# Second pass's loads of tokens and normed tokens issued by GpSimd instead of SyncE

## The chip, the cores and the metric

The kernel runs on one core of one Trainium2 chip. The metric is the device time of one execution in microseconds (us). Of the kernel before the change three timed executions are shown, 3959.48 to 3974.03 us, with a median of 3963.63 us, and one further execution that the hardware profiler recorded.

## What is computed

The reference takes `x`, 32 images of 56 x 56 tokens with 128 channels in f32, through two "metaformer" layers, each a token mixer and an expert stage with residual adds:

```python
x = x + conv(_ln_c(x))          # batch norm over all tokens, sign, 3x3 convolution with signed weights
t = t + moe(_ln_t(t))           # 8 experts, the two with the highest gate, weighted by their gates
x = x + triangle(_ln_c(x))      # sigmoid products a, b per image; z = einsum(a, b); norm; gate
t = t + choice(_ln_t(t))        # 64 experts, each takes its 8 best tokens of an image and adds to them
```

The first mixer normalizes each token, then needs a mean and a variance over all tokens of all images. So the work has two passes over `x`: the first finds these sums, the second does everything else.

## The kernel before

**Tiling.** A unit is 896 tokens, a tile of 128 partitions x 7 x 128 f32 (448 KB). There are 112 units, 7 for each of 16 pairs of images.

**First pass.** SyncE loads each unit (L1552), DVE and ACT normalize it, PE transposes it and sums up its squares (L1594), and SyncE stores the transposed normed tokens to `y1_d` (L1585).

**Second pass**, in the terms of one pair of images:

- `fetch` loads a unit's tokens `x_` from the input again (L557). They stay in one of 12 slots "x" until the pair is done with them; the slot comes free when the last stage has read the tile and stored it to the output (`out<-x`, on ACT's queue).
- `sign` loads the unit's normed tokens `ys` back from `y1_d` (L565) into one of 5 slots "u", which many other tiles share; DVE compares them with a limit per channel and writes signs into a padded frame (L572).
- `conv` runs 9 matmuls per half unit on that frame (L594), ACT scales them (L602), PE turns them back (`trc`), and DVE adds them to `x_` (L536). This add is the first reader of the tokens.
- `moe_stats`, `moe_turn`, `moe_route` and `moe_gates` normalize the tokens, turn them, work out the eight gates of each token, and store the gates of a unit to HBM (`gate<-gT`, L769, on ACT's queue).
- `moe_experts`, once for each of a unit's 7 groups of 128 tokens: SyncE loads the group's 8 x 128 gates from HBM, broadcast to all 128 partitions (`gb`, 512 KB, L782, 784 of them, 5 slots "gb"); DVE multiplies them with the turned tokens (L788); PE multiplies the product with the eight experts' weights and sums up (L793); DVE adds the result to the tokens (L805).
- The triangle stage (L817 to L1037) and the last norm follow; ACT stores the finished tokens and the last norm's output `y3`; `top8` picks 8 tokens for each of 64 experts, and GpSimd gathers them from `y3` with 8 indirect DMAs for each pair (L1154, 64 KB each), which DVE sums up (L1172, L1174).

**Tail.** Once all pairs are routed, the 64 experts run on the chosen tokens; their weights come on SyncE's queue (L1319, L1323), and GpSimd adds the results into the output with 128 indirect DMAs in a row (L1418).

**Order.** All stages are entered in a list by `put` with a time each. The class `Order` then plays the list through with estimated durations, gives each operation to an engine when it is ready and a slot is planned to be free, and so fixes the order of the instructions of every engine. `@op("SP", 360, ..., land=1200)` enters an operation as one of SyncE's with its cost; the function under it issues the instruction, which may name another engine. On the chip each engine, SyncE and GpSimd included, goes through its own instructions in order: a DMA whose slot isn't free yet holds up the DMAs behind it on that engine.

Of the kernel before, what the change touches and what calls it, by code (L numbers as in the profile page):

```python
# [252 lines left out]
def kernel(ctx: ExitStack, tc: tile.TileContext, a: dict, out: bass.AP):  # L253
    nc = tc.nc
# [26 lines left out]
    def units(ap):  # L281

        return ap.rearrange("(u p n) c -> u p n c", p=128, n=N7)

    x_units = units(x.rearrange("b h w c -> (b h w) c"))
# [68 lines left out]
    y1_d = [dram.tile([C, N7, 128], F32, name=f"y1_{g}") for g in range(NUT)]  # L354
# [17 lines left out]
    with ExitStack() as c2:  # L372
# [26 lines left out]
        def new(tag, shape, name, dtype=F32):  # L399
            return op.tile(pools.get(tag, work), tag, shape, dtype, name)  # L400

        def unit_tile(name):
            return new("u", [128, N7, C], name)
# [4 lines left out]
        def parts(t, n=N7):  # L408
            return [(t, k) for k in range(n)]
# [4 lines left out]
        def rows_of(u):  # L414

            r0 = 16 * u
            if r0 < H < r0 + 16:
                return ((0, r0, H - r0, 0), (1, 0, r0 + 16 - H, 8 * (H - r0)))
            return ((r0 // H, r0 % H, 16, 0),)

        def bands(p, u):

            for h in range(2):
                img, r = divmod(2 * u + h, N7)
                yield ("frame", (2 * p + img) % NF, r)
# [125 lines left out]
        def fetch(p, u):  # L551
            g = p * NU + u
            x_ = live[p]["x", u] = new("x", [128, N7, C], f"x_{NUT + g}")

            @op("SP", 360, w=parts(x_), land=1200)
            def _():
                nc.sync.dma_start(x_.ap, x_units[g])  # L557

        def sign(p, u):
            g = p * NU + u  # L560
            y = unit_tile(f"ys_{g}")

            @op("SP", 360, r=[("y1_d", g)], w=[y], land=1200)
            def _():
                nc.sync.dma_start(y.ap, y1_d[g])  # L565

            keys = list(bands(p, u))
            for img, r0, nr, p0 in rows_of(u):
                @op("DVE", 80 + 60 * nr, r=[y, "bn"],
                    w=keys[: nr // 8] if p0 == 0 else keys[-(nr // 8) :])  # L570
                def _(img=img, r0=r0, nr=nr, p0=p0):
                    nc.vector.tensor_scalar(  # L572
                        frames[(2 * p + img) % NF][:, 1 + r0 : 1 + r0 + nr, 1 : 1 + W].rearrange(
                            "c r (v n) -> c r v n", n=N7
                        ),
                        y.ap[:, :, p0 : p0 + 8 * nr].rearrange("c n (r v) -> c r v n", v=NV),
                        bn_scale, bn_limit, ALU.mult, ALU.is_ge,
                    )
# [1319 lines left out]
```

## Time and profile before

| | us |
|---|---|
| median of 3 executions | 3963.63 |
| the profiled execution | 3960.44 |
| its span, first to last instruction | 3958.7 |
| PE busy (matmul) | 3579.1 (90%) |
| DVE busy | 3205.5 (81%) |
| ACT busy | 2318.1 (59%) |
| GpSimd (POOL) busy | 411.9 (10%) |
| DMA queue q1: 673.15 MB | 50.4% of 16 engines |
| DMA queue q10: 109.20 MB | 7.0% |
| DMA queue q0, software: 17.32 MB | 3.0% |

The first pass lasts until about 310 us, the second to about 3440 us, and the tail to the end. q1 is the queue that SyncE's DMAs use (it moves most of the bytes), and q0 the one of the indirect DMAs that GpSimd issues. In rows of the trace "PE acc L793 <- DVE gb L788: 51.3, 43, 3.0" says that PE stood before its instructions of line 793 until DVE's of line 788 were done, 51.3 us in all, 43 times, 3.0 us at the longest. "SPq" and "POOLq" are the issuing sequencers of SyncE and GpSimd. In a row of the timeline stand the start, the duration, the engine, the line, the operation and its tiles, and in square brackets the idle time before it and what ended it.

### The profile page before, as it was taken

The page shows a single profiled execution, that of the slowest core. Times are in us where ns is not written, and L with a number is a line of the kernel's source. Part 1 is how long each engine was busy: PE and PEld are TensorE (multiplying, and loading weights), DVE is VectorE, ACT ScalarE, POOL GpSimd, SP SyncE. Part 2 cuts the span into 40 slices and gives each one's busy share as a digit, 9 for nine tenths or more (in the row PEclk, how much of TensorE's full clock was granted, in tenths as well). Part 3 has the DMA queues.
Part 4 walks back from the last instruction along what each step waited for, and adds up shares of the span by engine and source line. Part 5 has one row for each costly group of instructions (what it writes and reads, how often), then busy time and mean ns, then how long its engine had stood idle before and what let it go on. Part 6 is the DMA issues. An engine that isn't in the chain of part 4 may idle for free. (4 is left out here: it accounts for less than half of the span.)

```text
span 3958.7 us, 77662 instructions
## 1 busy us (share of the span) xinstructions
PE 3579.1 (90%) x27571; PEld 2832.1 (72%) x27571; DVE 3205.5 (81%) x10496; ACT 2318.1 (59%) x5435; POOL 411.9 (10%) x441
## 2 busy tenths in 40 slices
PE   7998999999999999999999999999999999988563
PEld 6886877777777768686867777777777777765342
DVE  7997889898989888989898989888888898875311
ACT  5997356666656565656657574747474757454210
POOL 1000000001010101010101010101010101003657
PEclk8999999999999999999999999999999999988786
DMA  7996637474747465655556455656555555556784
GB/s 252 349 349 221 240 139 247 140 259 138 255 145 249 149 233 163 215 181 203 197 178 212 176 205 182 216 174 211 194 197 184 202 207 189 195 188 185 186 242 84
DMA packets 311396, 804.64 MB, mean 203 GB/s; under 512 B 71384, under 2 KB 95808, under 8 KB 311008
## 3 DMA queue, kind: packets, MB, share of 16 engines
q1 hardware_dynamic: 247888, 673.15, 50.4%
q10 hardware_dynamic: 41104, 109.20, 7.0%
q0 software_dynamic: 22016, 17.32, 3.0%
q8 instruction: 219, 3.59, 0.4%
q14 instruction: 169, 1.38, 0.1%
HBM read 629.33 MB, written 170.13 MB: 202 GB/s over the span
## 5 line engine op out<-in xcount | busy, mean ns | idle before, releaser
L793 PE MATMUL acc<-expert_w,gb 128*128 128x128 f32 x12544 | 1460.7, 278 | 56.0 <-DVE gb L788 51.3
L793 PEld LDWEIGHTS acc<-expert_w,gb 128*128 128x128 f32 x12544 | 1433.5, 194 | 99.1 <-DVE gb L788 65.2
L788 DVE TENSOR_TENSOR gb<-gb,xT 128x1024 f32<-128x1024 f32 x784 | 944.9, 1221 | 102.4 <-DMA gb<-gate 95.5
L449 DVE BATCH_NORM_STATS2 stln<-x 128x6 f32<-128x128 f32 x2352 | 587.3, 292 | 2.7
L1154 POOL DMA_INDIRECT rows<-y,near x128 | 182.9, 1429 | 3374.8 <-DMA gb<-gate 1444.0
L523 ACT ACTIVATE yl<-x,rmln 128x128 f32<-128x128 f32 x784 | 326.3, 492 | 213.2 <-DVE rmln L508 205.3
L594 PE MATMUL ps_cv<-frame,w_sign 128*128 128x448 bf16 x2016 | 423.1, 357 | 7.2 <-DVE frame L572 7.1
L523 ACT ACTIVATE yt<-x,rmln 128x128 f32<-128x128 f32 x784 | 324.3, 490 | 155.7 <-DVE rmln L508 151.7
L523 ACT ACTIVATE ym<-x,rmln 128x128 f32<-128x128 f32 x784 | 327.2, 496 | 92.4 <-DVE rmln L511 42.8
L594 PEld LDWEIGHTS <-w_sign 128*128 128x128 bf16 x2016 | 195.0, 98 | 189.1 <-issue 27.3
L1418 POOL DMA_INDIRECT out<-eo_False,picked x128 | 195.9, 1531 | 162.5 <-DMA out<-eo_False,picked 84.7
L995 PE MATMUL ps_g<-yT,wg 128*128 128x448 f32 x448 | 206.7, 566 | 1.7 <-DVE x L536 1.7
L523 ACT ACTIVATE y<-x,rm 128x128 f32<-128x128 f32 x448 | 196.2, 493 | 20.4 <-DVE rm L508 11.7
L544 ACT COPY xT<-trm 128x512 f32<-128x512 f32 x224 | 111.6, 543 | 158.3 <-PE trm L438 137.9
L449 DVE BATCH_NORM_STATS2 st<-x 128x6 f32<-128x128 f32 x784 | 182.1, 287 | 22.9 <-DMA x<-in_x 22.0
L1594 PE MATMUL gram<-y 128*128 128x128 f32 x1568 | 197.8, 279 | 0.0
L602 ACT ACTIVATE cv<-ps_cv,cv_shift,cv_scale 128x448 f32<-128x448 f32 x224 | 160.2, 725 | 60.3 <-PE ps_cv L594 53.0
L1594 PEld LDWEIGHTS gram<-y 128*128 128x128 f32 x1568 | 193.9, 199 | 0.0
L805 DVE TENSOR_TENSOR x<-acc,x 128x512 f32<-128x512 f32 x224 | 139.1, 621 | 65.3 <-PE acc L793 63.7
L1031 DVE SCALAR_TENSOR_TENSOR sg<-ps_zo,bz,sg 128x224 f32<-128x224 f32 x448 | 180.1, 450 | 13.3 <-PE ps_zo L1021 13.3
L1005 ACT ACTIVATE sg<-ps_g,bg 128x448 f32<-128x448 f32 x224 | 138.4, 634 | 83.5 <-PE ps_g L995 49.1
L438 PE MATMUL tr<-ident,y 128*128 128x128 f32 x784 | 140.6, 297 | 29.7 <-ACT y L523 24.6
(228 smaller groups left out, 5281.0 us busy)
## 6 DMA issues: line engine op xcount, KB each, us to landing
gb<-gate SPq DMA_DIRECT2D x784, 512.0 KB
x<-in_x SPq DMA_DIRECT2D x224, 448.0 KB
y<-yT SPq DMA_DIRECT2D x112, 448.0 KB
ys<-y SPq DMA_DIRECT2D x112, 448.0 KB
out<-x ACTq DMA_DIRECT2D x112, 448.0 KB
y<-yl ACTq DMA_DIRECT2D x112, 448.0 KB
w_False<-in_L_ffn_weight SPq DMA_DIRECT2D x128, 256.0 KB
w_True<-in_L_ffn_weight SPq DMA_DIRECT2D x48, 256.0 KB
```

Source lines behind the costliest of these rows:

```text
L438: nc.tensor.transpose(ps.ap[:, n * 128 : (n + 1) * 128], get()[:, n0 + n, :], ident)
L449: nc.vector.bn_stats(st.ap[:, c0 + k, :], src.ap[:, k, :])
L523: nc.scalar.activation(dst.ap[:, k, :], src.ap[:, k, :], AF.Identity, bias=m, scale=r)
L594: nc.tensor.matmul(acc, lhsT=w_sign[:, tap, :], rhs=frames[f][:, 8 * band + kh : 8 * band + kh + 8, kw : kw + W], start=(tap == 0), stop=( ...
L602: nc.scalar.activation(cv.ap[:, :, 64 * h : 64 * h + 64], ps.ap[:, :448].rearrange("c (q n) -> c n q", n=N7), AF.Identity, bias=cv_shift, ...
L788: nc.vector.tensor_tensor(gb.ap, gb.ap, over(xT.ap[:, n, :], E0), ALU.mult)
L793: nc.tensor.matmul(acc.ap[:, n % 4 * C : (n % 4 + 1) * C], lhsT=gb.ap[:, e, :], rhs=expert_w[:, e * C : (e + 1) * C], start=(e == 0), stop ...
L995: nc.tensor.matmul(psg.ap[:, :448], lhsT=wg, rhs=yT[:, H * img + r0 : H * img + r0 + 8, :].rearrange("c r w -> c (r w)"), start=True, stop ...
L1031: nc.vector.scalar_tensor_tensor(part, psz[q].ap[:, :224].rearrange("c (m v) -> c m v", v=2), bz, part, ALU.add, ALU.mult,)
L1154: nc.gpsimd.indirect_dma_start(out=rows.ap[:, j, :], out_offset=None, in_=y3_d[p], in_offset=bass.IndirectOffsetOnAxis(ap=near.ap[:, k + j ...
L1418: ins = nc.gpsimd.indirect_dma_start(out=tokens_out, out_offset=bass.IndirectOffsetOnAxis(ap=picked[lot][:rows, e : e + 1], axis=0), in_=e ...
L1594: nc.tensor.matmul(gram.ap[:, :C], lhsT=y.ap[:, n, :], rhs=y.ap[:, n, :], start=(g % G16 == 0 and n == 0), stop=(g % G16 == G16 - 1 and n ...
```

## The change

Two lines of the second pass change the engine that issues the load. The planner's entry for each stays as it was ("SP", 360, land=1200), so the planned order of all operations is the same; the 112 loads of `x_` and the 112 of `ys` stand in GpSimd's instruction order, among the 128 gathers of L1154, and no longer in SyncE's. SyncE issues the broadcasts of the gates, the small transfers of the routed tokens, and the last stage's weights.

```diff
         def fetch(p, u):
...
             @op("SP", 360, w=parts(x_), land=1200)
             def _():
-                nc.sync.dma_start(x_.ap, x_units[g])
+                nc.gpsimd.dma_start(x_.ap, x_units[g])
...
         def sign(p, u):
...
             @op("SP", 360, r=[("y1_d", g)], w=[y], land=1200)
             def _():
-                nc.sync.dma_start(y.ap, y1_d[g])
+                nc.gpsimd.dma_start(y.ap, y1_d[g])
```

## The prediction

> **What bounds the kernel now.** I read the stretches first, to find the part that the change can touch. The moved loads run from 310 us (first x load) to 3433 us (last one). The columns are the stretch, its length, then busy us of PE, PEld, DVE, ACT and POOL, the granted clock, the DMA share and GB/s.
>
> ```profile
> 1000.00:1600.00 600.00, 569.31 (x4495) 454.64 (x4493) 526.45 (x1630) 368.10 (x829) 36.70 (x24) 0.99 0.57 194
> 1600.00:2200.00 600.00, 565.01 (x4444) 450.43 (x4443) 523.06 (x1607) 366.48 (x829) 37.03 (x24) 0.98 0.58 197
> 3600.00:3959.00 359.00, 202.44 (x1255) 132.93 (x1253) 94.00 (x273) 69.28 (x130) 225.81 (x295) 0.76 0.72 187
> ```
>
> See: in the second pass PE works 565 to 570 of 600 us, DVE some 525, DMA 57%. PE is the bound, DVE close behind, and what can be won is PE's idle time: from 400 to 3440 us, 3040 less 2879 busy, **161 us**. The tail after 3600 us (POOL's scatters) holds none of the moved loads and only shifts.
>
> Next, who ends these idle times, and where SyncE's queue (SPq) stands, in the window 400 to 3440 us (us in total, times, longest):
>
> ```profile
> PE acc L793 <- DVE gb L788: 51.3, 43, 3.0
> PE trg L758 <- DVE gg L744: 19.9, 17, 1.6
> ...
> DVE gb L788 <- DMA gb<-gate: 86.0, 99, 3.2
> ```
>
> ```profile
> SPq L782 <- PE acc L793: 755.6, 433, 5.0
> SPq L782 <- DMA gate<-gT: 387.8, 57, 19.8
> SPq L557 <- ACT yl L523: 364.1, 77, 12.0
> SPq L782 <- DVE gb L788: 209.8, 77, 7.8
> SPq L557 <- DMA out<-x: 204.1, 32, 20.9
> SPq L565 <- PE trc L438: 135.3, 12, 13.8
> ```
>
> See: a third of PE's idle time is the chain broadcast (gb) late, DVE late, PE late; 51.3/86.0 = **0.60** of what DVE waits for gb arrives at PE. I use that share for every DVE wait below. SyncE stands over 1000 us at the moved loads (these rows and the smaller ones of L565), with gb's issues queued behind. But gb itself waits for one of its five slots (755.6 + 209.8 us) or for the gates' store (387.8 us), so most of that time a freed queue would only wait at its own head.
>
> **The change part by part.** PE's, DVE's and ACT's streams keep every instruction in the same order; 224 issues leave SyncE's queue and stand in GpSimd's, in their old order among themselves, between the 128 gathers of L1154. No byte is added.
>
> (1) *What gb gains.* I went through the timeline for each wait of DVE at L788 and noted what SyncE issued last before that gb. Behind another gb: 69.1 us, nearly all of it with the issue 0.03 us after the slot came free, so five slots and the transfer's own 4.6 us set it, not the queue. Behind an x load (L557): 26.0 us in 18 waits; behind a ys load (L565): 1.9 us. One of them:
>
> ```profile
> 1017.60 0.33 SPq L557 DMA_DIRECT2D x<-in_x  x1
> 1018.28 1.21 DVE L788 TENSOR_TENSOR gb<-gb,xT 128x1024 f32<-128x1024 f32 x1
> 1018.38 0.32 SPq L782 DMA_DIRECT2D gb<-gate  x1
> ...
> 1022.47 1.23 DVE L788 TENSOR_TENSOR gb<-gb,xT 128x1024 f32<-128x1024 f32 x1 [1.46 <-DMA gb<-gate]
> ```
>
> The gb goes out right behind an x load and DVE loses 1.46 us. If these 27.9 us go, PE wins 27.9 x 0.60 = **17 us**. At most all of L788's waits go: 51 us. At least it is a loss: the same bytes still share 16 DMA engines, and on two queues a gb that used to be ahead of a load now runs beside it. Queue q1 moved 673.15 MB in 50.4% of 16 engines' span, 337 GB/s, so a load of 448 KB is 1.36 us of all engines; 99 of the window's 753 gb are waited for (13%), so 200 loads x 1.36 x 0.13 x 0.60 = 21 us lost if each delays one gb by its whole length. I take 17, the row nearest to the matter; the ends are +51 and -21.
>
> The Trainium skill, DMA: Bandwidth & Descriptors, section Issuing engines are not separate DMA queues, speaks against the change: DMAs of any issuing engine run on the same 16 engines, and several issuers save only issue time. By it alone the sum would be the 224 issues of 0.33 us that SyncE no longer makes, at best a few us, since SyncE is no bound.
>
> (2) *What the moved loads lose.* A direct load issued by GpSimd is not in this trace. Nearest is its gather of 64 KB, against SyncE's x load of 448 KB where it is waited for:
>
> ```profile
> 1391.27 0.33 SPq L557 DMA_DIRECT2D x<-in_x  x1
> ...
> 1395.23 1.16 DVE L536 TENSOR_TENSOR x<-trc,x 128x512 f32<-128x512 f32 x2 [0.20 <-DMA x<-in_x]
> ```
>
> ```profile
> L1154 POOL DMA_INDIRECT rows<-y,near x128: 942/1018/4459, 696.7 to 3727.9; - x128
> ...
> DMA to landing us min/median/max: 2.5/3.4/6.0
> ```
>
> SyncE's load is there 3.96 us after its issue. A gather lands 2.5 / 3.4 / 6.0 us after it starts; 384 KB more at 337 GB/s add 1.2 us: 3.7 / 4.6 / 7.2 us. Load by load I took the time from issue to first reader (the add L536 for x, the frame pass L572 for ys): medians 48 and 9.9 us, but 15 x loads (about one a pair) have 3.95 to 6.9 us, and 23 ys loads 4.9 to 7.2 us. Those go out when their slot comes free, so a free queue does not help them. Summing what each lacks: landing at 3.7 us costs DVE nothing, at 4.6 us 3.1 us, at 5.4 us 12.4 us (ys 1.0, x 11.4), at 6.6 us 38.7 us, at 7.2 us 57.9 us. Times 0.60 at PE: 0 to **35 us**. I take 5.4 us, between median and worst because a gather's issue is often stretched (mean 1429 ns against a median of 1018): 7 us. The cover of the other 186 loads is the DVE work between issue and reader; without it each would cost what it lacks, as the 38 do.
>
> (3) *GpSimd's engine.* 224 issues of 1.43 us are 320 us on an engine that is busy 412 of 3959: free by itself. It can be held up, though:
>
> ```profile
> 1302.98 3.57 POOL L1154 DMA_INDIRECT rows<-y,near  x1 [0.31 <-issue]
> 1306.86 0.94 POOL L1154 DMA_INDIRECT rows<-y,near  x1 [0.30 <-issue]
> ```
>
> The 3.57 us one lies beside a run of L788 on DVE, the 0.94 us one beside two short DVE ops of 0.2 us. DVE's own ops do not suffer: L788 takes 1221 ns with and without a gather beside it. If the loads are stretched so, they land up to 2.6 us later, which is the 7.2 us end of (2) and is not added again.
>
> The Trainium skill, SBUF — State Buffer, section Who interferes with whom, says that a two-input VectorE op contends only with a GpSimd op that reads SBUF, and that the modes which would stop descriptor writing belong to copies and scalar ops. A gather reads its indices, a plain load reads nothing; by the rule the loads would keep the short issue and the landing stays near the median, a cost of 2 us. By the row alone it is up to 35.
>
> (4) *New order on GpSimd.* A load now stands behind gathers, which wait for the choice of rows (near) and the y3 stores. With the times of this trace only 5 of 224 loads went out before a gather that is now ahead of them, by 2.3 to 4.4 us; all five are ys loads with 11.0 to 14.4 us to their reader: cost 0, and 5 x 4.4 us at DVE if that cover were gone, 13 at PE. The other way round, a gather behind a load that waits for its slot holds up L1172/L1174 on DVE: no gather of this trace started before a load now ahead of it, so 0; if the planned order slips, its 34.6 us of waits for rows could double, 21 us at PE.
>
> (5) *Start and tail.* Around 310 to 400 us PE idles 10.6 us, where the x loads no longer stand between the y1 stores; the stores' rows wait for ACT, so 0, at most a few us won. The weights of the last stage stay on SyncE: 0.
>
> **Sum**, on the profiled execution (3960.4 us, span 3958.7 and 1.7 around it): 3960.4 - 17 + 7 = 3950 us, -0.3%. The median shown is 3963.6, 3.2 us above that execution, which I leave as it is.
>
> **Rivals.** *A, forecast:* both effects small, 3940 to 3960. *B, faster:* the queue was the whole trouble; slots are refilled so early that the knock-on waits go too. For it: over 1000 us of SyncE standing at loads. Against it: 69.1 of the L788 waits follow another gb. Price: 51 us less, 3909; two thirds of it, 3926. *C, slower:* software-issued loads land late at the slot-bound places, DVE waits at L536 and L572, and PE runs out of gb. For it: gathers up to 4.46 us in issue, 38 loads with under 7.2 us. Against: the median gather. Price: (2)'s 35 us with the gain kept at zero: 3995; with the sharing loss 4016. It decides once loads land later than 6.4 us after issue (33 us at DVE, 20 at PE, with no gain). *D, nothing arrives:* gb's waits are those of five slots and the freed queue waits for PE instead; loads keep their time: 3960.
>
> **Chances.** A 0.33, D 0.14, B 0.24, C 0.29. Below 0.5% (20 us) a measurement of this kernel can hardly tell a difference from none. So faster 0.24, same 0.46, slower 0.30: A and D lie within. The range runs from nearly all of B to nearly all of C, 3915 to 4010; A's own is 3935 to 3965.
>
> **What would show it.** (1) right: L788's wait for gb falls from 95.5 to about 65 us over the whole trace, and PE's at L793 from 51 to about 35; wrong if it stays or grows, then sharing has eaten it. (2) right: L536 and L572 wait some 10 to 15 us for DMA (now 3.0 and 1.4); C if 40 or more. (3): GpSimd's issue rows of L557 and L565 near 1 us, or stretched beside L788. (4): L1174 waits for rows about 35 us as now. The forecast falls if the new loads' landing is far from 5.4 us, or if PE's idle time in 400 to 3440 us changes elsewhere than at L793.

## The result, and the profile after

The changed kernel takes **3992.01 us** (median of 6 executions, 3989.14 to 3998.13) against 3963.34 us of the kernel before on the same chip (6 executions, 3957.58 to 3974.03): a ratio of 1.0067, with a 95% interval of 1.0054 to 1.0080. It is slower by 29 us. The forecast was 3950, on the other side.

The stretches of the kernel after, in the columns of before (us of the stretch, busy us of PE, PEld, DVE, ACT and POOL, granted clock, DMA share, GB/s); the last row begins at its own first scatter:

```profile
1000.00:1600.00 600.00, 568.01 (x4473) 454.55 (x4474) 525.40 (x1618) 365.84 (x825) 59.05 (x64) 0.98 0.58 196
1600.00:2200.00 600.00, 561.28 (x4407) 448.26 (x4408) 523.32 (x1611) 364.41 (x827) 58.55 (x65) 0.98 0.58 196
3627.00:3991.00 364.00, 206.59 (x1255) 134.19 (x1255) 94.91 (x275) 69.83 (x132) 225.83 (x295) 0.75 0.72 184
```

PE and DVE are as busy as before; only POOL has more to do. A fixed stretch can't show a loss that is spread thin, so I compare the same work in both: from the first MAX8 (L1112, one for each pair) to the fifteenth. First row the kernel before, second row after:

```profile
685.00:3530.60 2845.60, 2690.32 (x21138) 2135.87 (x21138) 2493.09 (x7705) 1737.69 (x3919) 167.08 (x112) 0.98 0.57 195
```

```profile
691.60:3558.10 2866.50, 2697.88 (x21139) 2147.61 (x21138) 2493.42 (x7705) 1735.19 (x3919) 268.25 (x298) 0.98 0.56 193
```

This part, "the fourteen pairs" from here on, takes 20.9 of the 32.9 us by which the span grew: PE has the same instructions and works 7.6 us longer on them, and idles 13.3 us more (168.6 for 155.3). Before the first MAX8 6.6 us are lost, after the fifteenth 5.4.

The waits of 400 to 3440 us, after (us in total, times, longest), against those of before in the prediction:

```profile
DVE gb L788 <- DMA gb<-gate: 88.9, 101, 3.2
...
PE acc L793 <- DVE gb L788: 48.9, 32, 3.5
...
PE trg L758 <- DVE gg L744: 19.4, 17, 1.6
...
DVE x L536 <- DMA x<-in_x: 12.8, 10, 1.7
...
PE ps_zo L1021 <- DVE x L536: 8.3, 8, 2.1
...
PE acc L793 <- issue: 6.6, 3, 2.3
```

```profile
SPq L782 <- DMA gate<-gT: 1132.0, 58, 39.7
SPq L782 <- PE acc L793: 832.6, 466, 5.0
SPq L782 <- DVE gb L788: 337.9, 86, 7.8
```

See: SyncE's queue is free of the loads and now stands at gb's own reasons (slots, the gates' store), 1132 us where it was 388. The sum of the waits for gb hasn't moved (88.9 for 86.0, and 98.6 for 95.5 over the whole trace). New is a wait for x at L536, 12.8 us where it was 3.0, and PE behind it.

Two things stand behind these rows. The three waits at L793 marked "issue" end 0.06 us after an L788 of DVE, so they are waits for L788 too: PE stands 55.5 us for it in all, where it was 51.3 (54.9 in a second profile of the kernel before). And the waits for gb changed places. By the order of SyncE's issues in the traces, a gb issued right behind a moved load was waited for 27.1 us before, and no such gb is left; a gb issued right behind another gb was waited for 63.6 us before and 94.3 us after. (These are waits over 0.15 us; the prediction's 27.9 and 69.1 us have shorter ones too, and the second also some 5 us behind SyncE's other transfers.)

### The profile page after: what moved, and what is told of

It reads as the page before. It is cut to its first block, busy times and chain, and to the rows that moved or that the text cites. A ratio compares the mean times of both kernels' runs of the same rounds, so it can differ in the third digit from the quotient of the medians.

```text
span 3991.6 us, 77849 instructions
## 1 busy us (share of the span) xinstructions
PE 3590.8 (90%) x27571; PEld 2843.3 (71%) x27571; DVE 3204.6 (80%) x10496; ACT 2315.4 (58%) x5435; POOL 536.4 (13%) x665
## 5 line engine op out<-in xcount | busy, mean ns | idle before, releaser
L793 PE MATMUL acc<-expert_w,gb 128*128 128x128 f32 x12544 | 1467.4, 279 | 62.3 <-DVE gb L788 48.9
L793 PEld LDWEIGHTS acc<-expert_w,gb 128*128 128x128 f32 x12544 | 1441.0, 195 | 103.9 <-DVE gb L788 62.1
L788 DVE TENSOR_TENSOR gb<-gb,xT 128x1024 f32<-128x1024 f32 x784 | 943.0, 1218 | 105.7 <-DMA gb<-gate 98.6
L557 POOL DMA_DIRECT2D x<-in_x x112 | 60.3, 539 | 1430.6 <-DVE q L469 300.8
L1154 POOL DMA_INDIRECT rows<-y,near x128 | 183.3, 1432 | 495.9 <-DVE x L805 189.0
L565 POOL DMA_DIRECT2D ys<-y x112 | 64.3, 574 | 1349.6 <-ACT ym L523 303.6
L995 PE MATMUL ps_g<-yT,wg 128*128 128x448 f32 x448 | 206.3, 564 | 3.3 <-DVE x L536 3.3
L523 ACT ACTIVATE y<-x,rm 128x128 f32<-128x128 f32 x448 | 195.4, 489 | 20.9 <-DVE rm L508 11.8
L602 ACT ACTIVATE cv<-ps_cv,cv_shift,cv_scale 128x448 f32<-128x448 f32 x224 | 159.6, 722 | 62.6 <-PE ps_cv L594 54.7
```

The source lines that it names most:

```text
L523: nc.scalar.activation(dst.ap[:, k, :], src.ap[:, k, :], AF.Identity, bias=m, scale=r)
L602: nc.scalar.activation(cv.ap[:, :, 64 * h : 64 * h + 64], ps.ap[:, :448].rearrange("c (q n) -> c n q", n=N7), AF.Identity, bias=cv_shift, ...
L788: nc.vector.tensor_tensor(gb.ap, gb.ap, over(xT.ap[:, n, :], E0), ALU.mult)
L793: nc.tensor.matmul(acc.ap[:, n % 4 * C : (n % 4 + 1) * C], lhsT=gb.ap[:, e, :], rhs=expert_w[:, e * C : (e + 1) * C], start=(e == 0), stop ...
L995: nc.tensor.matmul(psg.ap[:, :448], lhsT=wg, rhs=yT[:, H * img + r0 : H * img + r0 + 8, :].rearrange("c r w -> c (r w)"), start=True, stop ...
L1154: nc.gpsimd.indirect_dma_start(out=rows.ap[:, j, :], out_offset=None, in_=y3_d[p], in_offset=bass.IndirectOffsetOnAxis(ap=near.ap[:, k + j ...
```

## The experiments

Theories. **Landing:** the x load of each pair's unit 5 goes out when its slot comes free and is read a few us later ("the urgent load" from here on), and on GpSimd's queue it lands later. **Two queues:** bytes that stood in one line now run side by side, and something urgent is delayed by something that isn't. **Software path:** an issue by GpSimd is slower whatever it carries. **Start:** the loss before the first MAX8 is that of the first loads.

The lengths of "the fourteen pairs" are from one profile each. The kernel before, profiled again, has 2846.3 us for 2845.6. That is one repetition; the differences to before in this column and those of the medians disagree by up to some 10 us (g3: 25 and 35), so a few us in one profile are not read as an effect.

| run | on GpSimd's queue | time, us | ratio to before (95%) | fourteen pairs, us | L788 for gb | L536 for x |
|---|---|---|---|---|---|---|
| before | none | 3963 | 1 | 2845.6 | 95.5 | 3.0 |
| c0_before_again | none | 3964 | one execution | 2846.3 | 99.9 | 2.8 |
| after | all 224 | 3992 | 1.0067 (1.0054 to 1.0080) | 2866.5 | 98.6 | 12.8 |
| e1_x_only | 112 x | 3990 | 1.0058 (1.0040 to 1.0076) | 2877.0 | 93.6 | 15.2 |
| e2_ys_only | 112 ys | 3980 | 1.0034 (1.0021 to 1.0047) | 2865.8 | 105.8 | 10.5 |
| e3_x5_sync | all but x of unit 5 | 3997 | 1.0081 (1.0061 to 1.0101) | 2870.8 | 115.0 | 9.5 |
| e4_start_sync | all but the first 28 | 3987 | 1.0054 (1.0033 to 1.0075) | 2866.0 | 103.5 | 11.6 |
| e5_pair_sync | all but x of unit 5 and its ys | 3993 | 1.0076 (1.0058 to 1.0094) | 2869.2 | 117.8 | 2.5 |
| f1_cut_pool | all, cut to 1/7 | 3926 | 0.9906 (0.9888 to 0.9924) | 2798.9 | 65.5 | 2.1 |
| f2_cut_sync | none, cut to 1/7 | 3919 | 0.9891 (0.9871 to 0.9910) | 2798.7 | 61.5 | 0.3 |
| h1_paced_x | none, x in pieces | 4030 | 1.0156 (1.0141 to 1.0171) | 2914.0 | 68.2 | 53.9 |
| h2_paced_x_ys | none, x and ys in pieces | 4086 | 1.0310 (1.0296 to 1.0324) | 2953.5 | 61.7 | 28.0 |
| k1_paced_234 | none, x of 2, 3, 4 in pieces | 3958 | 0.9986 (0.9977 to 0.9995) | 2845.8 | 79.1 | 2.3 |
| j1_x_on_act | none, 112 x on ScalarE's | 3999 | 1.0098 (1.0077 to 1.0118) | 2871.7 | 75.1 | 11.2 |
| g1_small_packets | all, in thirds | 3992 | 1.0066 (1.0049 to 1.0084) | 2866.5 | 99.9 | 9.1 |
| g2_x234_pool | x of 2, 3, 4 | 3969 | 0.9996 (0.9985 to 1.0007) | 2842.5 | 86.6 | 2.0 |
| g3_x016_pool | x of 0, 1, 6 | 3999 | 1.0086 (1.0067 to 1.0104) | 2871.0 | 106.9 | 3.2 |
| g4_x5_pool | x of 5 | 3982 | 1.0050 (1.0032 to 1.0069) | 2857.6 | 96.9 | 15.2 |
| g5_ys_late_pool | ys, not of 1 | 3969 | 1.0014 (1.0001 to 1.0027) | 2856.1 | 112.8 | 1.5 |

The last two columns are DVE's waits over the whole trace, in us.

### Halves, the urgent load and the start

```diff
 # e1: x on GpSimd, ys back        # e2: the other way round
-nc.gpsimd.dma_start(y.ap, y1_d[g])
+nc.sync.dma_start(y.ap, y1_d[g])
 # e3
-nc.gpsimd.dma_start(x_.ap, x_units[g])
+(nc.sync if u == 5 else nc.gpsimd).dma_start(x_.ap, x_units[g])
 # e4, for x and for ys
+(nc.sync if g < 14 else nc.gpsimd).dma_start(...)
```

> The x loads (L557) on GpSimd's queue, the ys loads (L565) back on SyncE's. Landing theory (the loss comes from the x load of each pair's unit 5, which is slot-bound and lands later on GpSimd's queue): the loss stays nearly whole, 3983 to 3992 us, and DVE's wait for it at L536 stays near 12.8 us (3.0 before). Queue theory (gb lost its place in line because loads now run beside it): the loss is split by bytes, about half of it each in this run and in the one with ys alone, near 3977. Start theory (the first loads of the second pass go out late on GpSimd, 4 to 7 us of the loss): this run keeps it only if the x loads between the y1 stores cause it; by the trace it is the first ys loads, so about 5 us below the changed kernel.

> The ys loads (L565) on GpSimd's queue, the x loads (L557) back on SyncE's. Landing theory: nearly nothing of the loss is left, 3963 to 3970 us, with DVE's wait at L536 back near 3 us. Queue theory: about half of the loss, near 3977. Start theory: the 4 to 7 us at the beginning of the second pass are here, so first L788 some 4 us later than in the kernel before.

> As the changed kernel, but the x load of unit 5 of each pair (16 of 112, the ones that wait for their slot and are read within 4 to 9 us) is issued by SyncE. Landing theory: DVE's wait at L536 falls from 12.8 to about 3 us, the half-clock time between the first and fifteenth MAX8 falls from 126 to about 95 us, and the time from 3992 to 3970 to 3976 (the start's 4 to 7 us stay). Queue theory: 3988 to 3992, since 96 of 112 x loads and all ys loads still run beside gb. Start theory: 3985 to 3992.

> As the changed kernel, but all loads of the first two pairs' units (g under 14, x and ys: 28 of 224) are issued by SyncE. Start theory: the first L788, 3.6 us later in the changed kernel than before, comes back to within 1 us, and the time falls by 4 to 7 us, to 3985 to 3988. Landing theory: it falls by 1 to 2 us, for one of 14 slot-bound x loads (3990). Queue theory: 1/8 of the loss, 3988.

No theory passed whole. x alone costs nearly everything (24 us), ys alone half (14 us), so the halves don't add up. With the urgent load back on SyncE (e3) the time should have fallen and didn't. The trace says why: before, the ys load that goes out on the same slot release stood 0.5 us behind x in SyncE's queue; in e3 it is on the other queue, in six pairs it goes out 0.77 us ahead of x, and there x needs 0.8 to 2.0 us more from its issue to its landing than in the kernel before. DVE waits for it for 9.5 us in all, where it was 3.0 and 2.8. e4 gave back 5 us of 29, with intervals that overlap, and left the first MAX8 at 690.6 us (before 685.0, before again 687.2, after 691.6). The start theory isn't supported; what the 6.6 us are made of stays open.

### Bytes, the pair, and how steady the profile is

```diff
 # e5: e3, and the ys load of the same slot release
+(nc.sync if u == 1 else nc.gpsimd).dma_start(y.ap, y1_d[g])
 # f1 (GpSimd; f2 is the same on SyncE). The add L536 and the frame pass L572 are
 # changed too, to do without the parts that are left out (not shown)
+k = N7 if g < 14 else 1
+nc.gpsimd.dma_start(x_.ap[:, :k, :], x_units[g][:, :k, :])
+nc.gpsimd.dma_start(y.ap[:, :k, :], y1_d[g][:, :k, :])
```

> As the changed kernel, but the x load of unit 5 and the ys load that goes out on the same slot release (unit 1 of the next pair) both stay with SyncE, in their old order: 32 of 224 loads. With the x load alone on SyncE, DVE's wait at L536 stayed 9.5 us, since the ys load then ran beside it or ahead of it on the other queue. Theory of two queues (what one queue sends in turn, two send at once, and the urgent one lands later): the wait at L536 goes back to 3 to 4 us, and the time falls by the x part of the loss, to 3975 to 3985. Theory that the other 192 loads beside gb make the loss: still 3985 to 3995, with L536 at 3 to 4.

> As the changed kernel, but from the third pair on each moved load carries one of its seven parts (64 KB for 448 KB); the parts that are not loaded are not used: the frame is filled from the one part, and the add at L536 takes a constant in place of the tokens, which it overwrites, so it still waits for the load. To be read against the next run, the same cut with the loads on SyncE. Theory of two queues (bytes that run beside each other): the difference between the two shrinks with the bytes, from 28 us to under 8. Theory of the software path (issue and landing of a GpSimd load are slower whatever it carries): the difference stays above 15.

> The same cut to one part of seven with all loads on SyncE, as in the kernel before. With 86 MB less to move, gb waits less: if the loads ahead of gb cost what the prediction took (27.9 us of DVE's waits), the time falls to 3940 to 3950, and DVE's wait for gb at L788 to 65 to 70 us; if the five slots and gb's own transfer set these waits, it stays within 10 us of the kernel before, with L788 at 85 to 95.

> The kernel before once more, for a second profile: how far its waits and half-clock windows differ from execution to execution. If the 95 us of half clock between the first and fifteenth MAX8 are typical of it, this profile has 85 to 105; if its first profile was a lucky one, 115 or more, and then the clock is no part of the change's loss.

f1 and f2 are the clearest pair of the study. They leave out six of the seven parts of each moved load from the third pair on, so their output isn't the reference's. With a seventh of the bytes the two assignments of queues take 2798.9 and 2798.7 us for the fourteen pairs, and the medians differ by 7 us with intervals that overlap. So the 224 issues by GpSimd show no cost of their own: the software path alone is not the main cause, **the loss needs the bytes that run beside other bytes**. DVE's waits for gb, f1 and then f2:

```profile
DVE gb L788 <- DMA gb<-gate: 65.5, 76, 3.2
```

```profile
DVE gb L788 <- DMA gb<-gate: 61.5, 78, 3.1
```

On SyncE's queue as well the waits fall by 34 us when the bytes go, and those behind an x load from 25.8 to 1.8 us. The prediction's 27.9 us "behind a moved load" were real, and less to move takes them away. The change left every byte and altered the place alone, and DVE's sum for gb stayed. (The times of f1 and f2 are not to be held against the kernel before: the frame pass L572 reads one part again and again in them, and is 47 us faster over the fourteen pairs.)

e5 put L536 back to 2.5 us and lost as much elsewhere: L788 waits 117.8 us. The second profile of the kernel before has the same time at half the granted clock ("half-clock time") in the fourteen pairs as the first, 96 us; after has 126, and e1 to e4 have 123 to 143. So that difference is hardly the luck of one execution. It isn't a measure of the loss, though: k1, below, has 113 and no loss.

### Which loads

```diff
 # g2: u in (2, 3, 4)   # g3: u in (0, 1, 6)   # g4: u == 5
+(nc.gpsimd if u in (2, 3, 4) and g >= NX else nc.sync).dma_start(x_.ap, x_units[g])
 # g5
+(nc.gpsimd if u != 1 and g >= NX else nc.sync).dma_start(y.ap, y1_d[g])
 # g1: all on GpSimd, x and ys as
+[nc.gpsimd.dma_start(x_.ap[:, i:j, :], x_units[g][:, i:j, :])
+ for i, j in ((0, 2), (2, 4), (4, 7))]
```

> As the changed kernel, but each moved load is issued in three pieces (two, two and three of its seven parts), so that its packets are smaller. Theory of packets (a queue's share of an engine goes by the size of its packets, and the software queue's of 7168 bytes crowd out the broadcasts' of 4096): the broadcasts that go out shortly before a load land nearer to 6 us than to 7.9, L788's wait falls from 98.6 to 80 to 90 us, and the time by 5 to 15 us, while L536's wait stays or grows. Theory of mere company: the same bytes beside the same broadcasts, L788 within 5 us of 98.6 and the time within 6 us of 3992, or above it by the 448 further issues.

> Only the x loads of units 2, 3 and 4 (from the second pair on, 45 of the 224 loads; 62 to 107 us to their reader) on GpSimd's queue, all others on SyncE's. Nobody waits for these loads, so only what they do to the transfers beside them shows. Theory of mere company: the loss goes by bytes beside broadcasts, 45/224 of it, at most 6 us: 3962 to 3970, L536 near 3. If a load beside costs a broadcast less than a load ahead of it, the time falls as in the paced run, by 3 to 8 us, to 3955 to 3961, with L788 at 85 to 92.

> Only the x loads of units 0, 1 and 6 on GpSimd's queue (from the thirteenth unit on). They have 16 to 46 us to their reader. If only urgent transfers matter: as the run with units 2, 3 and 4, within 5 us of the kernel before. If a load beside a broadcast costs whatever its own slack: half of the loss of all x loads or more, 3975 to 3985, with L788's waits moved to other broadcasts.

> Only the slot-bound x load of unit 5 on GpSimd's queue, 15 of 224 loads, with the ys load of the same slot release on SyncE beside it. If the late landing of this load is the main loss: L536 waits 10 to 15 us for DMA (3 before), and 3978 to 3988. If it is one of several small ones: L536 as said, and 3967 to 3975.

> Only the ys loads of all units but 1 on GpSimd's queue (from the thirteenth unit on, 84 of 224 loads). They have 5 to 16 us to their reader. If the loss goes with loads that have little slack and so run beside the work that waits: 3970 to 3980, most of what all ys loads cost. If ys costs only through the pair with x of unit 5: within 4 us of the kernel before.

**g4 is the landing theory by itself:** 15 loads cost 18 us. In before SyncE issues this load 0.03 us after the yl pass that frees the slot, in 0.33 us, and by the DMA's semaphore it lands 4.52 us after the start of the issue (medians over the 15 loads; 4.35 in the second profile); in g4 GpSimd needs 0.30 us, 0.57 us and 5.65 us, in the changed kernel 0.29, 0.54 and 5.31. So the load is there 1.1 to 1.6 us later; 0.3 us of this is the later start and some 0.2 us the longer issue, and the runs don't divide the rest. The same place as the prediction showed for before, now in the changed kernel:

```profile
1401.10 0.54 POOL L557 DMA_DIRECT2D x<-in_x  x1 [11.69 <-DVE mk L700]
1401.63 0.54 POOL L565 DMA_DIRECT2D ys<-y  x1
1401.73 1.15 DVE L536 TENSOR_TENSOR x<-tro,x 128x512 f32<-128x512 f32 x2
1405.65 0.69 DVE L536 TENSOR_TENSOR x<-trc,x 128x512 f32<-128x512 f32 x1 [1.04 <-DMA x<-in_x]
```

1.04 us of waiting where it was 0.20. No earlier issue is possible: the slot isn't free until 0.29 us before it.

**g3 is the two-queue theory by itself**, and the dearest group, above the 3975 to 3985 us expected, though nobody waits for these loads (15.6 us to their reader at least, in before). It adds 11.4 us to L788, and nearly all of it falls on one broadcast, the nineteenth of each pair, last of a burst of four: 11.7 us where it was 1.4, in four pairs above all. The worst of them, first before, then g3, at the same work:

```profile
1196.71 0.34 SPq L557 DMA_DIRECT2D x<-in_x  x1
1197.10 2.31 SPq L782 DMA_DIRECT2D gb<-gate  x4
...
1203.10 0.33 SPq L557 DMA_DIRECT2D x<-in_x  x1
...
1206.69 0.33 SPq L557 DMA_DIRECT2D x<-in_x  x1
...
1210.69 1.23 DVE L788 TENSOR_TENSOR gb<-gb,xT 128x1024 f32<-128x1024 f32 x1 [0.88 <-DMA gb<-gate]
```

```profile
1198.36 0.34 SPq L557 DMA_DIRECT2D x<-in_x  x1
...
1198.75 16.25 SPq L782 DMA_DIRECT2D gb<-gate  x8
...
1204.99 0.58 POOL L557 DMA_DIRECT2D x<-in_x  x1 [89.72 <-DMA gb<-gate]
...
1208.19 0.56 POOL L557 DMA_DIRECT2D x<-in_x  x1 [2.62 <-ACT yl L523]
...
1215.54 1.22 DVE L788 TENSOR_TENSOR gb<-gb,xT 128x1024 f32<-128x1024 f32 x1 [4.03 <-DMA gb<-gate]
1216.82 0.30 PEld L793 LDWEIGHTS acc<-expert_w,gb 128*128 128x128 f32 x2 [2.36 <-DVE gb L788]
```

In both the pair's urgent x load and a burst of four broadcasts right behind it go out first, and two other x loads 4 to 10 us later. The fourth broadcast is issued at 1198.91 and 1200.75. By the trace's packet records, the first packet of the load behind the burst starts at 1208.7 before, 2 us before the burst's last broadcast is there. In g3 the packets of the two loads run on their own queue from 1208.8 to 1214.7, nearly all the time until that broadcast is there. It takes 14.8 us from its issue instead of 11.8. Two loads are 917 KB, 2.7 us at the 337 GB/s of the prediction. **A queue of its own is not only a way past others; it also lets a load that has time run beside the broadcast that has none.**

What this does to PE, in g3 over the whole trace:

```profile
PE acc L793 <- DVE gb L788: 59.6, 41, 4.0
...
PE acc L793 <- issue: 11.1, 4, 4.1
```

The second row is again waits that end 0.05 to 0.06 us after an L788. Together PE stands 70.7 us for L788 where it was 51.3 and 54.9 in the two profiles of before. In g3's fourteen pairs PE idles 18.2 us more than before, about as much as that, and the rest of their 25 us is PE's longer busy time.

The Trainium skill, DMA: Bandwidth & Descriptors, section Queues, rings and completion order, says that each DMA engine goes round the queues that have work for it, a packet from each in turn. The packets of both queues in the same stretch, and the 14.8 us for 11.8, agree with it. The runs don't show that the size of the packets sets the shares: g1 cut the moved loads' data packets from 64 of 7168 bytes to 112 of 4096 on average, and the time stayed (3992.4 for 3992.0).

g2 says the same from the other side: 42 loads (the expectation miscounted) with 62 us and more to spare change nothing on GpSimd's queue (0.9996), and L788's waits don't grow (86.6 us). g5's ys loads cost 17 us more at L788 and 5 us of time, between its two expectations. The groups together (-3 + 25 + 12 + 11 us over the fourteen pairs) exceed the whole (21): with the urgent load gone from SyncE's queue as well, the burst no longer stands behind it. In the pair shown the nineteenth broadcast lands 11.6 us after its issue in the changed kernel; L788 waits 0.8 us in all for this broadcast, and L536 waits instead. In e5 the urgent load is back ahead of the burst, and the nineteenth broadcast is waited for 10.3 us. That is how e5 could repair L536 and gain nothing.

### Another queue, and loads in pieces on one queue

```diff
 # j1: all loads but x on SyncE
+nc.scalar.dma_start(x_.ap, x_units[g])
 # h1: loads on SyncE; k1: the same for units 2, 3, 4 alone
+if u == 5 or g < NX:
+    nc.sync.dma_start(x_.ap, x_units[g])
+else:
+    PEND.extend((x_, x_units[g], k0, k1) for k0, k1 in ((0, 2), (2, 4), (4, 7)))
 # behind each gb's dma_start the next piece of PEND goes out on SyncE's queue;
 # ahead of a tile's reader all that is left of the tile (piece itself not shown)
+piece(nc)
 # h2 (not shown): h1, and each ys load as four parts at once and three behind the next gb
```

> The x loads on ScalarE's queue, a second hardware queue, the ys loads on SyncE's: against the x loads alone on GpSimd's, which took 3990. Theory of two queues: any second queue does the same, so 3985 or more, the x load of unit 5 lands late (L536 waits 9 to 15 us for it), and on top of that ACT stands at slots that aren't free and the gates' stores queue behind loads. Theory that GpSimd's software path makes the loss: L536 waits 2 to 4 us for DMA, and the time stays within 10 us of the kernel before unless ACT's own stalls, which the trace would show at L557, exceed that.

> All loads on SyncE as in the kernel before, but each x load that isn't urgent (not unit 5, not the first 12) goes out in three pieces, one behind each of the next three broadcasts of gates, so that no broadcast has more than 3/7 of a load ahead of it. Theory that the bytes of a load ahead of a broadcast are what costs (28.8 us of DVE's waits in the kernel before, 4.9 with the loads cut to a seventh): L788's wait falls from 95.5 to 75 to 85 us and the time by 10 to 25 us, to 3940 to 3955. Theory that all that counts is the sum of bytes near the broadcasts, wherever they stand: within 5 us of the kernel before.

> As the run before, and each ys load in two pieces as well: four of seven parts at once, three behind the next broadcast. If pacing helps, L788 gains another 3 to 8 us, against frames that come later (L572 waited 1.4 us; up to 10 us if the second piece is late): 3935 to 3960. If pacing does nothing, as the kernel before or up to 10 us slower by the late frames.

> As the run with paced x loads, but only units 2, 3 and 4 are paced: their x loads have 62 to 107 us to their reader in the kernel before, so a late piece stops nobody, and 3/7 of the x loads are 43% of that run's gain at L788 (27.3 us): about 12 us. Theory that bytes ahead of a broadcast cost and the paced run lost only by late pieces: L788 waits 82 to 90 us, L536 stays near 3, and the time falls by 6 to 20 us, to 3947 to 3960. Theory that the loads' place beside the broadcasts does not matter as long as they are on one queue: within 5 us of the kernel before.

j1: a hardware queue delays the urgent load as well (L536 11.2 us), as two queues should. gb gained 20 us there, which GpSimd's queue didn't give: the 25.8 us behind x loads are gone, and those behind another gb stay at 66.4 (85.2 in e1, with the same loads on GpSimd's queue). So at gb the prediction's gain did come on another queue; at PE it didn't, L793 stands 53.6 us for L788. The kernel still lost 32 us, for a reason of its own that I had expected only in part: ACT's instructions come later, and DVE's waits at L740 for ACT's `d` grow from 21.6 to 54.7 us. Why gb does better beside ScalarE's queue than beside GpSimd's stays open; g1 speaks against packet size, the candidate.

h1 did to gb what was expected (95.5 to 68.2) and lost 62 us: pieces that wait for the next broadcast came late, those of unit 1 above all, which have the least time to their reader (50.7 of L536's 53.9 us). Its waits:

```profile
PE acc L793 <- DVE gb L788: 84.2, 41, 5.9
DVE gb L788 <- DMA gb<-gate: 68.2, 91, 3.1
DVE x L536 <- DMA x<-in_x: 53.9, 30, 5.1
```

See: PE's wait "for gb" grows by 33 us while DVE's wait for gb shrinks by 27. The row says only that L788 was late; what grew ahead of it on DVE is the wait at L536. h2 adds 106 us of waits at L572 and the same follows. k1, pieces only for loads with time, is the fastest kernel of the study that computes the reference: 0.9986 of before (0.9977 to 0.9995), 5 us, beneath the 6 to 20 expected, though L788 waits 16 us less, more than the 12 expected. Its profile shows none of the 5 us (2845.8 us for 2845.6), and PE's wait for L788 falls by 2 us alone, to 49.2 with the rows marked "issue".

## Why the prediction was wrong

**(1), the gain of gb, is the step that failed.** "If these 27.9 us go, PE wins 27.9 x 0.60 = 17 us": DVE's sum did not fall. L788 waits 98.6 us, where 65 would have shown the step right, and PE stands 55.5 us for it, where 35 was forecast. The waits behind a moved load did go, and the waits behind another broadcast took their place (63.6 to 94.3 us). I found what stood ahead of the waiting broadcast and took its place in the queue for the whole cause, while f2 shows that its bytes are what costs. The sum had the counter-term, a load that runs beside a gb, as an end of the range (-21 us) and put it at nothing in the forecast. Even that price was too low for some loads: 200 of them were to cost 21 us, and g3's 43 alone cost 25 us over the fourteen pairs. Beyond that, even the gain would have been small: k1 takes 16 us of waits off L788 and wins 5. Why GpSimd's queue gave gb nothing and ScalarE's 20 us stays open.

**(2), the late loads, was right in its time and wrong in its price.** Landing was taken at 5.4 us and is 5.3 (median over the 15 urgent loads); L536 and L572 wait 15.0 us for DMA, where 10 to 15 was forecast. The factor 0.60 from L793 doesn't hold at L536. There g4 adds 12.2 us of waits and loses 12.0 us over the fourteen pairs, 18 by the medians: PE waits for this add directly (L1021 behind L536: 10.6 us in g4, 8.3 in the changed kernel), and part of what is lost isn't idle time at all:

```profile
590.60:594.00 3.40, 1.50 (x18) 1.11 (x18) 2.91 (x12) 1.58 (x4) 0.00 (x0) 1.00 0.73 286
594.00:597.40 3.40, 0.96 (x5) 0.96 (x6) 3.26 (x12) 0.00 (x0) 0.00 (x0) 0.50 0.72 212
597.40:600.80 3.40, 3.40 (x22) 1.84 (x20) 3.33 (x12) 0.00 (x0) 0.00 (x0) 0.50 1.02 376
600.80:604.20 3.40, 3.37 (x37) 2.93 (x37) 3.40 (x7) 0.64 (x1) 0.00 (x0) 1.00 0.89 330
```

```profile
594.90:598.30 3.40, 1.50 (x18) 1.11 (x18) 2.12 (x9) 1.46 (x5) 0.00 (x0) 1.00 0.90 311
598.30:601.70 3.40, 0.00 (x0) 0.00 (x0) 3.40 (x13) 0.70 (x2) 0.00 (x0) 0.51 0.40 148
601.70:605.10 3.40, 2.45 (x19) 2.12 (x23) 3.19 (x14) 0.00 (x0) 0.00 (x0) 0.50 0.86 329
605.10:608.50 3.40, 3.40 (x19) 1.92 (x13) 3.40 (x12) 0.63 (x1) 0.00 (x0) 0.50 0.99 388
```

These are stretches of 3.4 us around the urgent load of the second pair, before and after; the clock is the third column from the right. DVE waits 0.8 us longer at L536 (1.28 for 0.49), PE's long wait there is 4.96 us for 4.17, and PE gets half its clock for three stretches instead of two. Over the fourteen pairs half-clock time grows from 96 to 126 us, and PE's busy time, for the same instructions, by 7.6 us (10.9 against the second profile of before): a third of the loss there or more. No term of mine had the clock. Of the 13.3 us that PE idles more, 8.2 are at L1021 and L995 behind L536 (11.6 for 3.4); L793's growth behind L788, 4.2 us, is about what the two profiles of before differ by (3.6).

**(3)** was wrong by size and harmless: an issue takes 0.54 us, not 1.43, and isn't stretched:

```profile
L557 POOL DMA_DIRECT2D x<-in_x x112: 536/536/744, 312.5 to 3461.3; - x112
...
L1154 POOL DMA_INDIRECT rows<-y,near x128: 940/998/5430, 703.3 to 3756.7; - x128
```

Gathers among the same instructions of DVE still go up to 5.43 us, x loads stop at 0.744. The Trainium skill, SBUF — State Buffer, section Who interferes with whom, as the prediction weighed it, agrees with these rows.

**(4)** was right: L1174 waits 30.4 us for rows, as against 34.6.

**(5)**, start and tail at nothing: the profile has 6.6 and 5.4 us there. The first MAX8 stands at 685.0 and 687.2 us in the two profiles of the kernel before and at 689.8 in g2, whose moved loads begin at 652, and the part after the fifteenth takes 426 to 438 us over all the profiles of the study, none of which moves a load there. So most of it can't be told from chance.

**The rivals.** What came is C's mechanism at a lower threshold, with D's half on gb: the freed queue stands at its own head, and gb gains nothing. C was to decide at 33 us of waits at L536 and L572; 15 were enough, since the gain it had to beat wasn't there, each us that L536 added cost PE more than 0.60 of idle time, and the half clock came on top. That bursts are delayed beside loads is shown in g3 and e5; in the changed kernel itself little of its loss is seen there.

## What to carry to other kernels

In these runs one queue was an order of precedence: before a load moves to a queue of its own, look at what is already in flight when it goes out, since from then on it shares with that instead of standing behind it. What is waited for behind a load is to be split into place and bytes, by a run that cuts the bytes, before a move is credited with it. A wait's price at the bottleneck belongs to the place of the wait, and where the granted clock falls after a stall, as it did here, the stall costs itself and then some of what comes after it.

## What the runs showed of the hardware

- A wait of GpSimd for another engine's semaphore ends 0.29 us after the event, SyncE's 0.03 us (medians over 15 loads each, after the yl pass); together with issue and landing the urgent x load of 448 KB is there 1.1 to 1.6 us later by GpSimd than by SyncE (0.3 us of it the wake-up; 5.31 and 5.65 us from issue to landing in the changed kernel and g4, against 4.52 and 4.35 in the two profiles of before).
- A load of 128 rows of 3584 bytes is 144 packets on SyncE's queue, 128 rows and 16 more, and 80 on GpSimd's, 64 of 7168 bytes and 16 more: two rows share a packet there. (With 224 loads moved, q1 loses 32256 packets and q0 gains 17920.)
- PE's clock fell to half after a stretch of 3.4 us in which PE was still busy for 1.50 us, as the first two rows of both clock fences show; the stall didn't fill a whole stretch.
